# Two graph-attention layers on one core: masks of whole tiles compared in layer 0's stage, and layer 1's sums copied in one piece with the source of tiny weight as a row below the identity

## The chip, the cores and the metric

The kernel runs on one core of one Trainium2 chip. The metric is device time in microseconds, the median of several runs. Beside it there is one profiled execution with a trace of every engine: TensorE (PE, with its weight loads PEld), VectorE (DVE), ScalarE (ACT), GpSimd (POOL) and SyncE (SP), which here only issues transfers.

## The reference, cut to what matters

`x` is 2708 x 256 and `adj` 2708 x 2708, sparse, with a full diagonal; the rows and columns of low number hold the most entries. Layer 0 mixes each node's neighbours through attention heads and two gated cells. Layer 1, where the change is, is an attention over 4 heads of 64 channels:

```python
h = (x @ W).reshape(n, HEADS, C)
s_src = jnp.einsum('nhc,hc->nh', h, a_src)
s_dst = jnp.einsum('nhc,hc->nh', h, a_dst)
e = jax.nn.leaky_relu(s_src[:, None, :] + s_dst[None, :, :], NEG_SLOPE)
e = jnp.where((adj > 0.5)[:, :, None], e, MASK_VAL)
alpha = jax.nn.softmax(e, axis=0)
out = jnp.einsum('ijh,ihc->jhc', alpha, h).reshape(n, HEADS * C) + bias
...
x = _layernorm(x + out)
```

A node j with no `adj > 0.5` in its column gets the mean of all h, since its softmax is over equal values.

## The kernel before, in words

**Sparse tiles.** Columns of `adj` are cut into spans, 64 wide for layer 0 and 128 wide for layer 1 (22 spans, the last 20 wide). For each span a first stage finds which rows have an entry, and lists them. A span's work is a list of items: a few whole tiles (rows m x 128 to m x 128 + 127, taken as they lie, `WHOLE1`) and tiles of 128 listed rows, gathered by indirect transfers from POOL (`TILES1`). `work1` holds 111 items: 91 gathered and 20 whole ones, four of them for the first two spans, whose last two row blocks are taken whole.

**Layer 0's stage.** A loop over `work0` fetches `adj` values (`fetch_raw`) and rows of the table `T0` (`fetch_rows`), scales them (`prepared`), multiplies (`multiplied`), and after each 512 columns runs the gated cells and the normalization (`cells_and_norm`), which also writes rows of h, scaled by exp of the source's logit, to the table `T1`. At item 40 of this loop the masks of layer 1's gathered tiles are fetched too: `fetch_mask`, line 1231, gathers 128 x 128 of `adj` into one of six `raw1` buffers, and DVE compares it with 0.5 into `m1`, one byte an entry.

**Layer 1's stage.** For each item, `fetch_h` (line 1312) brings 128 rows of `T1`, and for a whole tile also 128 x 128 of `adj` over SP's queue. `weighed` (line 1325) compares that tile with 0.5 on DVE into a bf16 mask, and computes for each head the weights `q = max(S, row's value) * mask` with one `scalar_tensor_tensor`. `S` is a span's share of the destination's factor on all partitions, copied by ACT into PSUM (`near`, line 1302). `attended` multiplies on PE: for each head 128 rows x 65 columns of h (64 channels and the weight itself, so the 65th row of the product is the denominator) into one of four PSUM banks.

**The end of a span.** `finished` (line 1364): ACT moves the bank to SBUF with four activations (one a head), each adding a bias by partition, `least_h`: 1e-20 times the mean of h, and 1e-20 for the denominator. This is a source of tiny weight, which decides only for a node without neighbours. PE turns the four 65 x 128 pieces into 128 x 65 with transposes, DVE takes the reciprocals of the denominators (`den`), ACT scales (`y`, four pieces), and DVE and ACT do the residual and the normalization in turn (`less`, `var`, `f_rstd`, `away`), before SP stores 128 rows of the result.

**What sets the order.** Nothing is issued as the loops run. `Plan` (line 99) records every operation with what it reads and writes, gives it an assumed cost, and `issue` (line 230) then places the operations one after another on the engines, each time the ready one with the longest tail of work behind it. So each engine's queue is in the planner's order, and an operation added in one place can move others. [...] All lines of the profile read L219, since the planner issues everything from there; the names of the tiles tell the operations apart. Tiles cut from common memory show under its name: `f_home` stands for layer 0's large buffers and in layer 1's stage for `q`, `o` and `S`; `f_m` for `m1`; `m` also for a whole tile's mask; `pl` and `ls` for the PSUM copies of `S`; `side` for the two PSUM banks of short products.

`kept` (line 862) are three 128 x 512 tiles through which products of the first stage go to memory (`XH`); they are not used after the first 261 us.

Of the kernel before, what the change touches and what calls it, by code (L numbers as in the profile page):

```python
# [10 lines left out]
F32 = mybir.dt.float32  # L11
BF16 = mybir.dt.bfloat16
I32 = mybir.dt.int32
U8 = mybir.dt.uint8
AF = mybir.ActivationFunctionType
ALU = mybir.AluOpType
# [4 lines left out]
P = 128  # L21
D = 256
KD = D // P
HEADS0 = 3
HEADS1 = 4
C1 = D // HEADS1
# [4 lines left out]
CH = 512  # L31
# [6 lines left out]
LEAST1 = 1.0e-20  # L38
# [6 lines left out]
W1 = 128  # L45
# [263 lines left out]
def fast_path(ctx: ExitStack, tc: tile.TileContext, i: dict, out: bass.AP, bad: bass.AP):  # L309
# [11 lines left out]
    nc = plan = Plan(tc.nc)  # L321
    x, xT_in, adj, adjT = i["x"], i["xT"], i["adj"], i["adjT"]
# [3 lines left out]
    size = [min(P, N - b * P) for b in range(NB)]  # L326
# [7 lines left out]
    TW = D + 8  # L334
    C65 = C1 + 1
# [13 lines left out]
    const = ctx.enter_context(tc.tile_pool(name="f_const", bufs=1))  # L349
# [3 lines left out]
    def ring(tiles):  # L353

        return cycle(tiles).__next__
# [29 lines left out]
    ident = const.tile([P, P], F32, name="f_ident")  # L385
# [64 lines left out]
    for t, of in ((less_room, TILES0 + TILES1), (less_whole, WHOLE0 + WHOLE1)):  # L450
        c = 0
        while c < len(of):
# [4 lines left out]
            c = e  # L457

    least = const.tile([NB, 1], F32, name="f_least")
# [62 lines left out]
    w1 = const.tile([P, KD, D + 2 * HEADS1], F32, name="f_w1")  # L522
# [8 lines left out]
    idx1 = const.tile([P, len(TILES1), max(TILES1)], I32, name="f_idx1")  # L531
# [5 lines left out]
    m1 = const.tile([P, sum(TILES1), W1], U8, name="f_m1")  # L537
    small, lists = Rings(const, 2), Rings(const, 2)
# [117 lines left out]
    def gathered(dst, table, idx, at):  # L656
        nc.gpsimd.indirect_dma_start(
            dst, None, table, bass.IndirectOffsetOnAxis(ap=idx, axis=0), element_offset=at
        )

    work0, work1 = [], []
# [21 lines left out]
    def fetch_raw(n):  # L683

        c, whole, m = work0[n]
        d0, w = spans[0][c]
        home, at = raw_home(n)
        raws[n] = home[:, at * W0 : at * W0 + w]
        if whole:
            nc.sync.dma_start(raws[n], adjT[m * P : (m + 1) * P, d0 : d0 + w])  # L690
        else:
            gathered(raws[n], adjT, idx0[:, c, m : m + 1], d0)
# [11 lines left out]
    for h in range(HEADS0):  # L704
        for k in range(KD):
            nc.vector.scalar_tensor_tensor(
                junk, gat_w[:, h, k, :], 1.0, a_b[:, 2 * h * D : (2 * h + 1) * D],
                op0=ALU.mult, op1=ALU.mult, accum_out=uw[:, k, h : h + 1],
# [137 lines left out]


    kept_bank = ring([accs[1], dbs[1]])
    keptp = Rings(const, 3)

    def place_kept(g, n, o, gate):
        at = (((g * 2 + n) * KD + o) * 3 + gate) * P
# [21 lines left out]
    for g, cs in enumerate(groups):  # L874
        w = width[g]
        pe, pf = accs[0], dbs[0]
        c0, nf = base[g] // W0, w // W0
        for b0 in range(0, NB, 2):
# [13 lines left out]
            whole = size[b0 + 1] == P  # L892
# [11 lines left out]
            for b in pair:  # L904
                if b in cs:
                    p, o = size[b], b * P - base[g]
# [16 lines left out]
            for b in pair:  # L923
                p = size[b]
# [3 lines left out]
            for b in pair:  # L928
                p = size[b]
# [37 lines left out]
    rowp, sp = Rings(const, 9), Rings(const, 4)  # L967
# [4 lines left out]
    rows, ready = {}, {}  # L972
# [253 lines left out]
    slot1 = {}  # L1226
    for n, (c, whole, m) in enumerate(work1):
        if not whole:
            slot1[n] = len(slot1)

    def fetch_mask(n):
        c, whole, m = work1[n]
        d0, w = spans[1][c]
        r = small.tile([P, W1], F32, name="raw1", bufs=6)
        gathered(r[:, :w], adj, idx1[:, c, m : m + 1], d0)
        nc.vector.tensor_scalar(m1[:, slot1[n], :w], r[:, :w], 0.5, None, op0=ALU.is_gt)

    for n, (c, whole, m) in enumerate(work0):
        if n == EARLY:
            for k in slot1:  # L1240
                fetch_mask(k)
        fetch_raw(n)
        fetch_rows(n)
        prepared(n)
        if multiplied(n):
            divided(c)
            d0, w = spans[0][c]
            if d0 + w in (base[g] + width[g] for g in range(NG)):
                cells_and_norm(d0 // CH)
# [17 lines left out]
    qp, op = Rings(const, 4, home4), Rings(const, 2, home2[:, 4 * CH :])  # L1267
# [4 lines left out]
    xmean = const.tile([P, KD], F32, name="f_xmean")  # L1272
# [1 line left out]
    nc.vector.tensor_scalar(xmean, xmean, 1.0 / N, None, op0=ALU.mult)  # L1274


    least_h = const.tile([C65, HEADS1], F32, name="f_least_h")
    nc.vector.memset(least_h, LEAST1)
    pm = side()
    for h in range(HEADS1):  # L1280
        for k in range(KD):
            nc.tensor.matmul(
                pm[:C1, h : h + 1], lhsT=w1[:, k, h * C1 : (h + 1) * C1], rhs=xmean[:, k : k + 1],
                start=(k == 0), stop=(k == KD - 1), skip_group_check=True,
            )
    nc.vector.tensor_scalar(least_h[:C1], pm[:C1, :HEADS1], LEAST1, None, op0=ALU.mult)

    def on_all_partitions(g):
        S_b = next_S()
# [7 lines left out]


    near_bank = ring([pl_bank(), ls_bank()])

    def near(c):
        d0, w = spans[1][c]
# [7 lines left out]
    hrows, hready, outs, of_g, of_c = {}, {}, {}, {}, {}  # L1310

    def fetch_h(n):
        c, whole, m = work1[n]
        d0, w = spans[1][c]
        hg, r = rowp.tile([P, TW], F32, name="rows"), None
        if whole:
            p = size[m]
            r = small.tile([P, W1], F32, name="raw1")
            nc.sync.dma_start(hg[:p], T1[m * P : m * P + p, :])
            nc.sync.dma_start(r[:p, :w], adj[m * P : m * P + p, d0 : d0 + w])  # L1320
        else:
            gathered(hg, T1[: (NB - LATE) * P, :] if c < SPLIT else T1, idx1[:, c, m : m + 1], 0)
        hrows[n] = (hg, r)

    def weighed(n):
        c, whole, m = work1[n]
        d0, w = spans[1][c]
        late = whole and m >= NB - LATE
        if (c, late) not in of_c:
            of_c[c, late] = near(c)  # L1330
        S = of_c[c, late]
        hg, r = hrows[n]
        p = size[m] if whole else P
        if whole:
            mask = small.tile([P, W1], BF16, name="m2")[:p, :w]
            nc.vector.tensor_scalar(mask, r[:p, :w], 0.5, None, op0=ALU.is_gt)
        else:
            mask = m1[:, slot1[n], :w]
        q = qp.tile([P, HEADS1, W1], F32, name="q")
        for h in range(HEADS1):  # L1340
            nc.vector.scalar_tensor_tensor(
                q[:p, h, :w], S[:p, h, :w], hg[:p, H65 + h : H65 + h + 1], mask,
                op0=ALU.max, op1=ALU.mult,
            )
        hready[n] = q

    def attended(n):

        c, whole, m = work1[n]
        w = spans[1][c][1]  # L1350
        start = c not in outs
        stop = n == ends1[c]
        p = size[m] if whole else P
        if start:
            outs[c] = out_bank()
        q, hg = hready.pop(n), hrows.pop(n)[0]
        for h in range(HEADS1):
            nc.tensor.matmul(
                outs[c][:C65, h * W1 : h * W1 + w], lhsT=hg[:p, h * C65 : (h + 1) * C65], rhs=q[:p, h, :w],
                start=start and h == 0, stop=stop and h == HEADS1 - 1, skip_group_check=True,  # L1360
            )
        return stop

    def finished(c):
        p = size[c]
        o = op.tile([C65, HEADS1, W1], F32, name="o")
        out_c = outs.pop(c)
        for h in range(HEADS1):
            nc.scalar.activation(
                o[:, h, :p], out_c[:C65, h * W1 : h * W1 + p], AF.Identity, bias=least_h[:, h : h + 1]  # L1370
            )
        pt = side()
        for h in range(HEADS1):
            nc.tensor.transpose(pt[:p, h * C65 : (h + 1) * C65], o[:, h, :p], ident[:C65, :C65])
        got = pt[:p, :H65].rearrange("p (h c) -> p h c", h=HEADS1)
        den = small.tile([P, HEADS1], F32, name="den")
        nc.vector.reciprocal(den[:p].rearrange("p (h o) -> p h o", o=1), got[:, :, C1:])
        y = small.tile([P, HEADS1, C1], F32, name="y")
        for h in range(HEADS1):
            nc.scalar.activation(y[:p, h, :], got[:, h, :C1], AF.Copy, scale=den[:p, h : h + 1])  # L1380
        y = y[:p].rearrange("p h c -> p (h c)")

        less = small.tile([P, 1], F32, name="less")[:p]
        var = small.tile([P, 1], F32, name="var")[:p]
        away = small.tile([P, 1], F32, name="away")[:p]
        scale = rstd[:p, c : c + 1]
        nc.vector.scalar_tensor_tensor(
            xn[:p, c, :], xn[:p, c, :], 1.0, y, op0=ALU.mult, op1=ALU.add, accum_out=less
        )
        nc.vector.tensor_scalar(less, less, -1.0 / D, None, op0=ALU.mult)  # L1390
        nc.scalar.activation(y, xn[:p, c, :], AF.Square, bias=less, accum_out=var)
        nc.scalar.activation(scale, var, AF.Sqrt, bias=eps[:p], scale=1.0 / D)
        nc.vector.reciprocal(scale, scale)

        nc.vector.tensor_mul(away, less, scale)
        nc.scalar.activation(
            xn[:p, c, :], xn[:p, c, :], AF.Identity, bias=away, scale=scale
        )
        nc.sync.dma_start(out[c * P : c * P + p, :], xn[:p, c, :])
# [461 lines left out]
```

## Time and profile before

| | |
|---|---|
| median of 3 runs | 1038.06 us (1037.52 to 1051.02) |
| profiled execution | 877.66 us |
| its span, first to last instruction | 875.8 us |
| mean granted TensorE clock in it | 0.959 |
| PE, DVE, ACT, POOL busy | 780.4, 609.9, 551.3, 532.3 us |
| layer 1's stage | from about 715 us to the end |

The profiled execution is 160 us shorter than the median of the runs. In the profile's rows a busy time is followed by the mean length of one instruction in ns and then the idle time of the engine just before it with what ended it. Instructions overlap somewhat with the next on the same engine, so that a length is more than an instruction's share of the engine's time. In the timeline and the chain the first number is the start and the second the length, both in us.

### The profile page before, as it was taken

The numbers are of one execution on the slowest core, as the hardware profiler recorded it, in microseconds if no ns is written. First come the engines' busy times: TensorE is split into PE (matmuls) and PEld (weight loads), VectorE is DVE, ScalarE is ACT, GpSimd is POOL, SyncE is SP. The second block draws the span as 40 slices with busy tenths as digits, with TensorE's granted clock in tenths as the row PEclk, the third lists the DMA queues.
The fourth block names the chain that finished last, engine by engine and source line by source line (L and its number), as shares of the span: only waits on it lengthen the run. The fifth ranks groups of instructions, "written<-read, shape, count | busy, mean of one in ns | idle before, by whom it ended". The sixth has DMA issues, their size and how long they took to land. (4 is left out here: it accounts for less than half of the span.)

```text
span 875.8 us, 14092 instructions
## 1 busy us (share of the span) xinstructions
PE 780.4 (89%) x3911; PEld 490.4 (56%) x3911; DVE 609.9 (70%) x2063; ACT 551.3 (63%) x1560; POOL 532.3 (61%) x613
## 2 busy tenths in 40 slices
PE   4999998997999999988998997999999899998882
PEld 3533333444556764656555744754664588777761
DVE  6259585865846674978478638727857849999993
ACT  3368997975568885658456844745764432237887
POOL 3000557557667777777777777777776243677630
PEclk9989999998999999989999999999999799999995
DMA  9476887878683342453446425434534143565531
GB/s 345 135 236 209 277 263 241 288 242 243 204 235 98 106 128 56 135 147 105 112 143 198 126 65 159 126 96 118 159 103 123 29 141 94 172 187 171 169 98 53
DMA packets 88503, 138.71 MB, mean 158 GB/s; under 512 B 21904, under 2 KB 44264, under 8 KB 87776
## 3 DMA queue, kind: packets, MB, share of 16 engines
q1 hardware_dynamic: 67168, 90.56, 32.2%
q0 software_dynamic: 20320, 45.59, 19.7%
q10 hardware_dynamic: 928, 1.57, 0.5%
q8 instruction: 33, 0.54, 0.3%
q14 instruction: 54, 0.44, 0.2%
HBM read 116.18 MB, written 24.26 MB: 160 GB/s over the span
## 5 line engine op out<-in xcount | busy, mean ns | idle before, releaser
L219 POOL DMA_INDIRECT rows<-f_T,f_idx x254 | 258.0, 1016 | 115.9 <-PE acc L219 26.8
L219 PE MATMUL acc<-four,rows 128*128 128x256 f32 (+1 forms) x712 | 187.9, 400 | 8.8 <-ACT four L219 5.7
L219 ACT ACTIVATE four<-four,rows 128x64 f32<-128x64 f32 (+1 forms) x534 | 143.3, 336 | 23.0 <-DMA rows<-f_T,f_idx 15.8
L219 PEld LDWEIGHTS acc<-four,rows 128*128 128x128 f32 x712 | 131.6, 196 | 45.8 <-ACT four L219 14.2
L219 POOL DMA_INDIRECT raw<-in_adj_dram,f_idx x91 | 90.5, 995 | 40.7 <-DVE f_m L219 15.3
L219 POOL DMA_INDIRECT f_xn<-in_adjT_dram,f_idx x63 | 66.8, 1060 | 20.1 <-issue 16.6
L219 POOL DMA_INDIRECT f_home<-in_adjT_dram,f_idx x67 | 66.4, 991 | 20.3 <-issue 16.3
L219 PE MATMUL acc<-f_home,rows 128*65 128x128 f32 (+2 forms) x512 | 65.2, 279 | 3.9 <-ACT f_home L219 2.6
L219 DVE TENSOR_TENSOR f_home<-f_home,side 128x512 f32<-128x512 f32 (+1 forms) x64 | 41.9, 658 | 32.4 <-PE side L219 31.2
L219 PEld LDWEIGHTS acc<-f_home,rows 128*65 128x65 f32 (+1 forms) x512 | 55.7, 140 | 9.6 <-ACT f_home L219 3.5
L219 PE MATMUL side<-f_home,f_gat_w 128*128 128x512 f32 (+1 forms) x144 | 58.7, 569 | 2.0 <-DVE f_home L219 1.9
L219 PE MATMUL side<-f_home,f_node_wi 128*128 128x512 f32 (+1 forms) x144 | 59.1, 543 | 1.3 <-DVE f_home L219 1.3
L219 ACT ACTIVATE m<-four 128x64 bf16<-128x64 f32 (+1 forms) x181 | 40.2, 246 | 28.1 <-DVE four L219 24.0
L219 PE MATMUL side<-f_home,f_edge_wi 128*128 128x512 f32 (+1 forms) x144 | 57.4, 544 | 0.0
L219 DVE SCALAR_TENSOR_TENSOR f_home<-pl,rows,f_m 128x128 f32<-128x128 f32 x196 | 55.2, 335 | 0.0
L219 POOL DMA_INDIRECT f_m<-in_adjT_dram,f_idx x33 | 31.9, 967 | 37.3 <-DVE f_rel L219 20.1
L219 PE MATMUL db<-f_home,rows 128*65 128x128 f32 x376 | 48.8, 282 | 6.3 <-DVE f_home L219 4.0
L219 DVE SCALAR_TENSOR_TENSOR f_home<-ls,rows,f_m 128x128 f32<-128x128 f32 (+1 forms) x168 | 46.3, 331 | 2.8 <-DMA rows<-f_T,f_idx 1.7
L219 PEld LDWEIGHTS db<-f_home,rows 128*65 128x65 f32 x376 | 39.0, 137 | 13.9 <-DVE f_home L219 5.9
L219 DVE TENSOR_REDUCE f_found<-f_home 128x16 f32<-128x1024 f32 (+8 forms) x52 | 43.7, 860 | 3.3 <-POOL f_home L219 3.3
L219 ACT ACTIVATE f_home<-f_home,f_minus_half 128x1024 bf16<-128x1024 f32 (+5 forms) x44 | 41.9, 965 | 5.8 <-PE db L219 4.1
L219 PEld LDWEIGHTS side<-f_home,f_gat_w 128*128 128x128 f32 x144 | 28.0, 208 | 30.1 <-issue 27.1
(231 smaller groups left out, 1537.3 us busy)
## 6 DMA issues: line engine op xcount, KB each, us to landing
f_home<-in_adjT_dram SPq DMA_DIRECT2D x30, 512.0 KB
f_XH<-kept SPq DMA_DIRECT2D x60, 256.0 KB
f_home<-f_XH SPq DMA_DIRECT2D x60, 256.0 KB
f_node_wi<-in_adjT_dram SPq DMA_DIRECT2D x10, 512.0 KB
f_edge_wi<-in_adjT_dram SPq DMA_DIRECT2D x10, 512.0 KB
f_home<-f_TS SPq DMA_DIRECT2D x5, 1024.0 KB
rows<-f_T SPq DMA_DIRECT2D x33, 132.0 KB
rows<-f_T,f_idx POOLq DMA_INDIRECT x254
```

What stands on the lines that cost most here:

```text
L219: call = lambda: f(*args, **kwargs)
```

## The change

1. Masks of whole tiles: `fetch_mask` now runs for all 111 items of `work1`. For a whole tile it loads `adj` over SP's queue into the same six `raw1` buffers and compares into one byte an entry, in space cut from the `kept` tiles (now `kept_home`). `fetch_h` no longer loads `adj`, and `weighed` no longer compares.
2. Sums: `finished` copies the bank with one ACT copy of 65 x (4 x width) into one of two fixed `o` tiles, whose rows 64 to 95 are set to 1.0 beforehand. The copy overwrites row 64 and row 65 stays 1.0.
3. The source of tiny weight: `back_h` holds, for each head, the 65 x 65 identity and below it, in row 65, 1e-20 times the mean of h (and 1e-20 for the denominator). The transposes become plain products of `o` (66 rows) with `back_h` (66 rows), which turn the piece and add row 65 at once. The row is made as 1 x 256 by two products with `xmean` in place of eight, scaled by DVE into `least`, and brought to partition 65 by a transfer on SP's queue.

```diff
-    keptp = Rings(const, 3)
+    kept_home = const.tile([P, 3 * CH], F32, name="f_kept_home")
+    keptp = Rings(const, 3, kept_home)
...
+    m1_whole = [
+        kept_home[:, k * W1 // 4 : (k + 1) * W1 // 4].bitcast(U8) for k in range(len(work1) - len(slot1))
+    ]
+    masks1 = {}
+
     def fetch_mask(n):
         c, whole, m = work1[n]
         d0, w = spans[1][c]
-        r = small.tile([P, W1], F32, name="raw1", bufs=6)
-        gathered(r[:, :w], adj, idx1[:, c, m : m + 1], d0)
-        nc.vector.tensor_scalar(m1[:, slot1[n], :w], r[:, :w], 0.5, None, op0=ALU.is_gt)
+        p = size[m] if whole else P
+        r = small.tile([P, W1], F32, name="raw1", bufs=6)[:p, :w]
+        if whole:
+            nc.sync.dma_start(r, adj[m * P : m * P + p, d0 : d0 + w])
+            masks1[n] = m1_whole.pop()[:p, :w]
+        else:
+            gathered(r, adj, idx1[:, c, m : m + 1], d0)
+            masks1[n] = m1[:, slot1[n], :w]
+        nc.vector.tensor_scalar(masks1[n], r, 0.5, None, op0=ALU.is_gt)
...
-            for k in slot1:
+            for k in range(len(work1)):
                 fetch_mask(k)
...
-    least_h = const.tile([C65, HEADS1], F32, name="f_least_h")
-    nc.vector.memset(least_h, LEAST1)
+    back_h = op.tile([P, HEADS1, C65], F32, name="back_h", bufs=1)
+    nc.vector.memset(back_h[C1 : C1 + 32], LEAST1)
+    nc.vector.tensor_copy(
+        back_h[:C65], ident[:C65, :C65].rearrange("p (o c) -> p o c", o=1).to_broadcast([C65, HEADS1, C65])
+    )
     pm = side()
-    for h in range(HEADS1):
-        for k in range(KD):
-            nc.tensor.matmul(
-                pm[:C1, h : h + 1], lhsT=w1[:, k, h * C1 : (h + 1) * C1], rhs=xmean[:, k : k + 1],
-                start=(k == 0), stop=(k == KD - 1), skip_group_check=True,
-            )
-    nc.vector.tensor_scalar(least_h[:C1], pm[:C1, :HEADS1], LEAST1, None, op0=ALU.mult)
+    for k in range(KD):
+        nc.tensor.matmul(
+            pm[:1, :D], lhsT=xmean[:, k : k + 1], rhs=w1[:, k, :D], start=(k == 0), stop=(k == KD - 1)
+        )
+    least = op.tile([1, HEADS1, C65], F32, name="least_h", bufs=1)
+    nc.vector.memset(least, LEAST1)
+    nc.vector.tensor_scalar(
+        least[:, :, :C1], pm[:1, :D].rearrange("p (h c) -> p h c", h=HEADS1), LEAST1, None, op0=ALU.mult
+    )
+    nc.sync.dma_start(back_h[C65 : C65 + 1], least)
...
+    o_tiles = [op.tile([P, HEADS1, W1], F32, name=f"o{k}", bufs=1) for k in range(2)]
+    for o in o_tiles:
+        nc.vector.memset(o[C1 : C1 + 32], 1.0)
+    next_o = ring(o_tiles)
...
     def fetch_h(n):
-        hg, r = rowp.tile([P, TW], F32, name="rows"), None
+        hg = rowp.tile([P, TW], F32, name="rows")
         if whole:
             p = size[m]
-            r = small.tile([P, W1], F32, name="raw1")
             nc.sync.dma_start(hg[:p], T1[m * P : m * P + p, :])
-            nc.sync.dma_start(r[:p, :w], adj[m * P : m * P + p, d0 : d0 + w])
...
     def weighed(n):
-        if whole:
-            mask = small.tile([P, W1], BF16, name="m2")[:p, :w]
-            nc.vector.tensor_scalar(mask, r[:p, :w], 0.5, None, op0=ALU.is_gt)
-        else:
-            mask = m1[:, slot1[n], :w]
+        hg, mask = hrows[n], masks1[n]
...
     def finished(c):
-        o = op.tile([C65, HEADS1, W1], F32, name="o")
-        out_c = outs.pop(c)
-        for h in range(HEADS1):
-            nc.scalar.activation(
-                o[:, h, :p], out_c[:C65, h * W1 : h * W1 + p], AF.Identity, bias=least_h[:, h : h + 1]
-            )
+        o = next_o()
+        out_c = outs.pop(c).rearrange("p (h j) -> p h j", h=HEADS1)
+        nc.scalar.copy(o[:C65, :, :p], out_c[:C65, :, :p])
         pt = side()
         for h in range(HEADS1):
-            nc.tensor.transpose(pt[:p, h * C65 : (h + 1) * C65], o[:, h, :p], ident[:C65, :C65])
+            nc.tensor.matmul(
+                pt[:p, h * C65 : (h + 1) * C65], lhsT=o[: C65 + 1, h, :p], rhs=back_h[: C65 + 1, h, :],
+                start=True, stop=True, skip_group_check=True,
+            )
```

More of the change, by code (lines that the diff above doesn't have):

```diff
@@ L1314, in fetch_h @@
         d0, w = spans[1][c]
-        hg, r = rowp.tile([P, TW], F32, name="rows"), None
+        hg = rowp.tile([P, TW], F32, name="rows")
         if whole:
             p = size[m]
-            r = small.tile([P, W1], F32, name="raw1")
             nc.sync.dma_start(hg[:p], T1[m * P : m * P + p, :])
-            nc.sync.dma_start(r[:p, :w], adj[m * P : m * P + p, d0 : d0 + w])
         else:
             gathered(hg, T1[: (NB - LATE) * P, :] if c < SPLIT else T1, idx1[:, c, m : m + 1], 0)
-        hrows[n] = (hg, r)
+        hrows[n] = hg
     def weighed(n):
@@ L1331, in weighed @@
         S = of_c[c, late]
-        hg, r = hrows[n]
+        hg, mask = hrows[n], masks1[n]
         p = size[m] if whole else P
-        if whole:
-            mask = small.tile([P, W1], BF16, name="m2")[:p, :w]
-            nc.vector.tensor_scalar(mask, r[:p, :w], 0.5, None, op0=ALU.is_gt)
-        else:
-            mask = m1[:, slot1[n], :w]
         q = qp.tile([P, HEADS1, W1], F32, name="q")
@@ L1355, in attended @@
             outs[c] = out_bank()
-        q, hg = hready.pop(n), hrows.pop(n)[0]
+        q, hg = hready.pop(n), hrows.pop(n)
         for h in range(HEADS1):
```

## The prediction

> **What bounds the kernel now.** I read first the span in 40 slices, to see which engine is full where.
>
> ```profile
> PE   4999998997999999988998997999999899998882
> DVE  6259585865846674978478638727857849999993
> ACT  3368997975568885658456844745764432237887
> PEclk9989999998999999989999999999999799999995
> ```
>
> PE is full through layer 0. From slice 33 (about 720 us) on it is DVE, and in the last three slices ACT rises. The busy times by stage say it sharper (columns: PE, PEld, DVE, ACT, POOL busy, granted clock, DMA share, GB/s):
>
> ```profile
> 715.00:840.00 125.00, 112.95 (x947) 97.55 (x946) 122.71 (x525) 59.55 (x187) 79.22 (x83) 1.00 0.54 162
> 840.00:852.00 12.00, 10.14 (x88) 8.54 (x87) 11.90 (x65) 12.00 (x49) 2.15 (x2) 1.00 0.27 80
> 852.00:870.00 18.00, 5.39 (x29) 3.62 (x28) 7.42 (x44) 17.67 (x72) 0.00 (x0) 0.57 0.17 59
> ```
>
> DVE works 134.6 of the 137 us to 852, ACT only half of the first 125 us and then all of the last 30. So layer 1 has two limits in a row: DVE until about 840, ACT after that. The chain that ended last agrees: from 837 us on it is nearly all ACT.
>
> ```profile
> 844.47 0.48 ACT pl L219
> 845.48 0.26 ACT f_home L219 x2
> 845.82 0.67 ACT f_home L219 x2
> 861.70 0.96 ACT f_home L219 x4
> 868.67 1.00 ACT f_xn L219 x2
> ```
>
> Four bias activations of one column (`f_home`, 845.48 and 845.82) hold ACT 0.93 us, and those of the last column, only 20 wide (861.70), 0.96; one copy of 512 wide (`pl`) holds it 0.48. Then the groups of the stretch from 715 us, with the rows that the change touches:
>
> ```profile
> L219 DVE SCALAR_TENSOR_TENSOR f_home<-pl,rows,f_m 128x128 f32<-128x128 f32 x194 | 54.5, 334 | 0.0
> L219 ACT ACTIVATE f_home<-acc,f_least_h 65x128 f32<-65x128 f32 x44 | 12.7, 391 | 5.2 <-DVE f_least_h L219 3.6 <-PE side L219 1.6
> L219 PE MATMUL side<-f_ident,f_home 65*128 65x65 f32 x84 | 11.3, 252 | 8.3 <-ACT f_home L219 5.3 <-ACT y L219 2.9
> L219 DVE TENSOR_SCALAR m<-raw 128x128 bf16<-128x128 f32 x15 | 3.0, 205 | 0.0
> ```
>
> The transposes are recorded once each (84 for 21 columns)[...]; the other fp32 products are recorded twice. Last the timeline, for what an instruction really takes of its engine when others follow:
>
> ```profile
> 741.89 0.34 DVE L219 TENSOR_SCALAR m<-raw 128x128 bf16<-128x128 f32 x2
> 712.25 0.37 DVE L219 SCALAR_TENSOR_TENSOR f_home<-side,f_edge_bh,f_home 128x148 f32<-128x148 f32 x1 [7.58 <-PE side L219]
> 101.62 1.05 PE L219 MATMUL side<-f_sum,f_home 9*128 9x3 f32 x8
> 766.19 0.41 PE L219 MATMUL side<-f_ident,f_home 65*128 65x65 f32 x4
> 766.43 1.04 PE L219 MATMUL acc<-f_home,rows 128*65 128x128 f32 x8
> ```
>
> Two mask comparisons start at 741.89 and the next instruction at 742.16: 0.135 us each, not the 0.205 of the row. Four transposes take PE 0.24 us (766.19 to 766.43). And DVE stands idle 7.58 us before 712.25.
>
> [...] the eight records above, with 9 rows, 128 weight columns and only 3 moving ones, take (1.05 - 0.25)/7 = 0.114 us each[...]
>
> **Whole-tile masks.** 20 loads of `adj` and 20 comparisons leave `fetch_h` and `weighed` and go to `fetch_mask`. Three of the comparisons are before 715 us now and bound nothing. The other 17 are in the full DVE stretch: 17 x 0.135 = 2.3 us off. Reading a U8 mask (`f_m`, 334 ns) costs `scalar_tensor_tensor` what a bf16 one (`m`, 336 ns) does: nothing. DVE gains in that stretch one scaling of 1 x 256 for the row of tiny weight; by the 128 x 256 `tensor_scalar` (two in 0.72 us) some 0.35, against 0.14 for `f_least_h` today: +0.2. The memsets of `o` and `back_h` and the copy of the identity (five, at most 0.3 us each) stand in the new order ahead of the last group's cell, in the 7.58 us of idle time: 0, or 1 us if that idle goes. Net on DVE: -2.1.
>
> In layer 0 the 20 come on top: 2.7 us of DVE, which is 60 to 75% busy there, and on SP 20 issues of 0.33 us. PE is the bound there. But a comparison waits for its load[...]:
>
> ```profile
> DVE f_m L219 <- DMA raw<-in_adj_dram,f_idx: 33.0, 17, 9.5
> SPq L219 <- DMA raw<-in_adj_dram,f_idx: 19.8, 2, 15.5
> ```
>
> 33.0 us over 91 gathered masks is 0.36 each, so 20 x 0.36 = 7.3 us of DVE waits at most, behind which `four` and the cells' DVE work are queued and, behind these, PE. PE waited for DVE 21 us in all from 400 to 720 us, for all reasons. I take +0.5, bounds 0 and +7. A gain is possible only through a luckier order; -2. The first of the new comparisons must also follow the last store of a `kept` tile (DVE's last such copy is at 257.7 us, the comparison would be at about 261): at most 1 us, inside those bounds.
>
> **One copy for four bias activations.** 22 columns; the copy as `pl` above (the PSUM copies `kept` are 0.57 long, the same) at 0.48 against 0.97 with the gap between two: 0.49 less each. The columns before 840 us save ACT time that it has to spare: 0. After 840 us the timeline has 24 of the bias activations of 128 wide, six columns, and the last column's four, with ACT never idle: 6 x 0.49, and 0.96 less about 0.15 for a copy of 80 elements (the last `ls` copy holds ACT 0.12), is -3.7. Bounds: 0 (the columns' chains take over) and 22 x 0.49 = -10.8 (every column counts).
>
> **Products for transposes.** Each of 88 transposes (0.24/4 = 0.06) becomes a plain fp32 product with 66 rows, 128 weight columns, 65 moving: two records of 0.114, as `side<-f_sum`. A column takes 0.91 instead of 0.24 us, +0.67; 22 columns +14.7 us of PE. Up to 852 us that is beside DVE: an item (four heads) takes PE 0.87 (765.32 to 766.19), with a fifth of a column 0.92 now, 1.05 then; DVE takes 134.6/109 = 1.23. So cover is there at the profile's clock of 1.00, 0. In the tail PE is busy 5.4 of 18 us, though at clock 0.57; the new order has other ACT work of over 3 us between a column's copy and its `y`. I charge +0.3; +2 if every one of the last columns waits.
>
> **The row of tiny weight.** Two products instead of eight (-0.8 us of PE, hidden), then a store from SBUF to SBUF[...]. PE meets the first product that needs it four items, 3.5 us, after `xmean`'s. 0; +2 at most, and four `q` buffers cover DVE. The activations no longer wait for `f_least_h`, which came only at 762.1; that frees accumulator banks earlier: 0.
>
> **Sum.** -2.1 + 0.5 - 3.7 + 0.3 = -5.0, for the profiled execution 877.7 (span 875.8) to about 873. The median of the runs is 1038.06, 160 us above the profile, so those runs were under other conditions than the trace shows. Had everything followed TensorE's clock, 0.959 x 877.7/1038 = 0.81 would do it. I carry the difference over unscaled: 1033.1.
>
> **Rivals.**
> - *PE becomes layer 1's bound in the timed runs (slower).* At clock k PE needs 1.05/k an item, DVE 1.21: PE decides below k = 0.87; before the change below 0.92/1.23 = 0.75. [...] At 0.81, (1.30 - 1.23) x 109 = +7.6, with the tail's -3.4 +4.2; at 0.785 +9. Against it: in the trace the clock is 1.00 in this stretch. Some 1044 (1040 to 1048).
> - *Masks stall layer 0 (slower).* SP holds its queue up to 15.5 us for a ring slot already; with `f_XH` loads and `f_T` stores behind it once more, PE would miss about 10: +5, 1043 to 1048.
> - *The tail is not ACT's* but the last column's chain: -2.1 alone, +2 for the products: about 1038 (1037 to 1040).
> - *All of ACT's saving counts*, since columns finish earlier: -2.1 - 10.8 = -13: 1025.
>
> **Chances.** Forecast 0.47 (its own range 1029 to 1037), PE's bound 0.26, stalls 0.07, no gain 0.10, large gain 0.10. From 1025 to 1048 holds some 0.82. 2%, about what a measurement of this kernel can tell from no change, is 1017.3 and 1058.8: only a clock that differs between the runs, or bounds added up, lead there: 0.05 faster, 0.05 slower, 0.90 within.
>
> **What would show it.** Right: no `m<-raw` after 715 us; DVE's last full-width product about 1 to 2 us earlier; ACT copies of 65 x 512 near 0.5 us and its last piece 4 to 6 us earlier; `side` products in eight records a column. Wrong: PE's waits in layer 0 up by over 5 us, SP held longer by raw loads, or DVE idle for PE in layer 1.

## The result, and the profile after

The median went from 1039.59 us (4 runs, 1037.52 to 1051.02) to **1052.22 us** (4 runs, 1049.99 to 1055.13): ratio 1.0101, 95% interval 1.0057 to 1.0145. Forecast were 1033.1 us and a range to 1048. That is within 2% of no change, but of the other sign than forecast and outside the range.

Two things have to be known to read the numbers: both kernels take about 880 us on some chips and about 1035 to 1050 us on others, with nearly the same busy times of DVE and ACT, some 50 to 60 us more of PE and more idle time of all; and a ratio leaves out executions more than 1.5% above the fastest of their kernel, so that it isn't exactly the quotient of the medians beside it. The profile of the kernel before (877.66 us) is of the first kind, and all times of this first comparison, with the profile after (1049.99 us, span 1048.2), of the second. So these two profiles may not be subtracted.

The 40 slices of the changed kernel, as shown of before:

```profile
PE   4989796968688876987798859696988787988894
DVE  5376547546535551977267506642852756988895
ACT  4468676825347671656337614462563332242467
PEclk9789989987899988989998878898988979999897
```

Everywhere engines are emptier, PE too, and the mean granted clock is lower (0.888 against 0.959). The busy times show it by stage. I cut both profiles where DVE forms the mean of x (`f_xmean`), just ahead of layer 1's sums: at 742.7 us before and 903.4 us after (columns: PE, PEld, DVE, ACT, POOL busy, granted clock, DMA share, GB/s). Before:

```profile
0.00:742.70 742.70, 679.03 (x3069) 404.89 (x3069) 495.22 (x1541) 470.61 (x1275) 462.10 (x540) 0.97 0.54 161
742.70:842.70 100.00, 87.43 (x741) 74.34 (x740) 98.09 (x432) 53.69 (x179) 70.25 (x74) 1.00 0.58 171
```

After:

```profile
0.00:903.40 903.40, 729.28 (x3068) 425.21 (x3069) 500.94 (x1559) 470.63 (x1275) 453.97 (x540) 0.88 0.45 133
903.40:1003.40 100.00, 86.48 (x686) 77.12 (x685) 85.30 (x356) 36.61 (x102) 60.13 (x64) 0.95 0.47 142
```

Layer 0 is 160.7 us longer, 93% of the difference between the spans, with the same work on ACT (470.6 us) and nearly the same on DVE; PE is busy 50 us longer (729.3 against 679.0). The chain that ended last names what had no place in the chain before, idle time that nothing recorded ends:

```profile
PE 58%; another core or an unknown queue 9%; ACT 9%; DVE 8%; issue 7%; ACTq 0%; DVEq 0%
```

And the rows that the change touches, in the groups of after:

```profile
L219 DVE SCALAR_TENSOR_TENSOR f_home<-pl,rows,f_m 128x128 f32<-128x128 f32 x196 | 55.7, 340 | 5.7 <-PE acc L219 4.4 <-remote 0.8 <-PE side L219 0.4
L219 PE MATMUL side<-f_home 66*128 66x65 f32 x168 | 23.3, 284 | 9.0 <-ACT y L219 5.4 <-issue 3.2 <-ACT f_home L219 0.3
L219 ACT COPY f_home<-acc 65x512 f32<-65x512 f32 x11 | 6.4, 579 | 12.4 <-PE side L219 4.3 <-PE acc L219 4.3 <-PE db L219 3.8
L219 DVE TENSOR_SCALAR f_kept_home<-raw 128x128 uint8<-128x128 f32 x18 | 4.2, 241 | 2.0 <-issue 2.0
```

The change did what it says: one ACT copy a column, products of 66 rows with two records each, masks compared into `f_kept_home`. But DVE, never idle ahead of the first of these groups before, now waits 5.7 us ahead of it. The wait alone doesn't speak against the change: the kernel before waits there too in the longer condition, as a later profile of it (the control below) shows:

```profile
L219 DVE SCALAR_TENSOR_TENSOR f_home<-pl,rows,f_m 128x128 f32<-128x128 f32 x196 | 55.8, 340 | 7.3 <-PE acc L219 3.0 <-PE side L219 2.7 <-PE db L219 1.6
```

### The profile page after: what moved, and what is told of

Its sections match the earlier page's. It is cut to its first block, busy times and chain, and to the rows that moved or that the text cites. A ratio compares the mean times of both kernels' runs of the same rounds, so it can differ in the third digit from the quotient of the medians.

```text
span 1048.2 us, 14160 instructions
## 1 busy us (share of the span) xinstructions
PE 843.3 (80%) x3987; PEld 527.6 (50%) x3987; DVE 616.0 (59%) x2067; ACT 540.3 (52%) x1494; POOL 523.9 (50%) x613
## 4 chain that ended last, share of the span: by engine, by line
PE 58%; another core or an unknown queue 9%; ACT 9%; DVE 8%; issue 7%; ACTq 0%; DVEq 0%
PE acc L219 25%; PE side L219 18%; PE db L219 13%; DVE f_home L219 4%; ACT four L219 3%; PE pl L219 2%; ACT f_home L219 2%; ACT y L219 1%; DVE four L219 1%; ACT ids L219 1%; PE ls L219 1%; DVE f_xn L219 1%; ACT f_xn L219 1%; DVE ids L219 0%
## 5 line engine op out<-in xcount | busy, mean ns | idle before, releaser
L219 POOL DMA_INDIRECT rows<-f_T,f_idx x254 | 252.6, 994 | 218.4 <-issue 42.3
L219 PE MATMUL acc<-four,rows 128*128 128x256 f32 (+1 forms) x712 | 201.1, 422 | 14.6 <-ACT four L219 9.3
L219 PEld LDWEIGHTS acc<-four,rows 128*128 128x128 f32 x712 | 140.2, 208 | 55.3 <-issue 20.5
L219 PE MATMUL side<-f_home,f_edge_wi 128*128 128x512 f32 (+1 forms) x144 | 70.6, 641 | 40.8 <-ACT f_home L219 21.6
L219 PE MATMUL acc<-f_home,rows 128*65 128x128 f32 (+1 forms) x512 | 69.5, 288 | 6.4 <-issue 5.8
L219 PEld LDWEIGHTS side<-f_home,f_edge_wi 128*128 128x128 f32 x144 | 29.8, 222 | 78.2 <-issue 32.6
L219 PEld LDWEIGHTS acc<-f_home,rows 128*65 128x65 f32 (+1 forms) x512 | 59.1, 145 | 13.0 <-issue 8.2
L219 PE MATMUL side<-f_home,f_node_wi 128*128 128x512 f32 (+1 forms) x144 | 61.3, 558 | 3.0 <-DVE f_home L219 3.0
L219 PE MATMUL db<-f_home,f_only 128*22 128x512 bf16 (+2 forms) x132 | 39.2, 388 | 20.7 <-ACT f_home L219 17.8
L219 ACT ACTIVATE f_home<-f_home,f_minus_half 128x1024 bf16<-128x1024 f32 (+5 forms) x44 | 41.9, 965 | 24.9 <-issue 19.5
L219 POOL DMA_INDIRECT f_m<-in_adjT_dram,f_idx x33 | 31.6, 957 | 38.8 <-DVE f_rel L219 20.1
```

The source lines that it names most:

```text
L219: call = lambda: f(*args, **kwargs)
```

## The experiments

### The two halves, on a chip where the kernel before takes 880 us

First the kernel before itself, without an edit, to see which of the two conditions is its own.

> The kernel before, unchanged, once more with a trace. If the timed runs of before were under the conditions of the changed kernel's trace (span 1048, clock 0.89, stalls in which DVE, ACT and PE all stand), this trace shows them too: span near 1037, clock below 0.92. If those stalls belong to the change, they are absent here and the span is near 876.

It took 881.19 us, span 879.4, beside 43 timed runs with a median of 880.56, and none of its waits is put down to an unknown releaser. So 1038 us isn't the kernel's own time, but the chip's or the occasion's.

The masks alone (the hunks on `keptp`, `fetch_mask`, `fetch_h` and `weighed`):

```diff
-            for k in slot1:
+            for k in range(len(work1)):
                 fetch_mask(k)
...
-        if whole:
-            mask = small.tile([P, W1], BF16, name="m2")[:p, :w]
-            nc.vector.tensor_scalar(mask, r[:p, :w], 0.5, None, op0=ALU.is_gt)
```

> Only the masks of whole tiles are moved to layer 0's stage; the four bias activations and the transposes stay. Theory PE (the plain products cost it): no slower than before, ratio 0.995 to 1.000. Theory masks (the loads and comparisons stall layer 0): ratio 1.008 to 1.012, as the whole change. Theory order (any new order of the queues can cost or give a per cent): anything from 0.99 to 1.01.

876.17 us (22 runs) against 880.56: **0.9959** (0.9934 to 0.9984). The sums alone (the hunks on `back_h`, `o_tiles` and `finished`):

```diff
-        for h in range(HEADS1):
-            nc.scalar.activation(
-                o[:, h, :p], out_c[:C65, h * W1 : h * W1 + p], AF.Identity, bias=least_h[:, h : h + 1]
-            )
+        nc.scalar.copy(o[:C65, :, :p], out_c[:C65, :, :p])
```

> Only the sums in one copy, the plain products and the row of tiny weight; the masks of whole tiles stay in layer 1's stage. Theory PE: ratio 1.008 to 1.015. Theory masks: 0.995 to 1.000. Theory order: anything from 0.99 to 1.01.

876.70 us against 880.56: **0.9973** (0.9948 to 0.9999). Each half gains; neither costs. Last the whole change without its products:

```diff
+        nc.scalar.activation(o[:C65, :, :p], out_c[:C65, :, :p], AF.Identity, bias=tiny)
...
+            nc.tensor.transpose(pt[:p, h * C65 : (h + 1) * C65], o[:C65, h, :p], ident[:C65, :C65])
```

> The whole change, but PE keeps transposes: one activation with a constant bias of 1e-20 copies the sums, and there is no row of tiny weight. Left out: the mean of h for a node without neighbours. Theory PE: some 15 us of PE gone against the change, ratio to before 0.993 to 0.998. Theory masks: 1.005 to 1.010, nearly as slow as the change. Theory order: no sign foretold.

0.9824 (0.9782 to 0.9867), from six runs only (862.30 to 880.06 us), an unclear comparison. The median of all six, 871.79 us, is 0.990 of 880.56. It is repeated below.

### The whole change, and TensorE's part alone

> The changed kernel unchanged. Theory A (the stalls seen in its first profile are conditions, not its own): where the kernel before takes about 880 us, the two halves add up to 0.9959 x 0.9973 = 0.993 of it, 874 us, and no layer-0 wait of 10 us stands in the trace; layer 1 from the first mean to the end is 129 to 132 us against 133 before. Theory B (the order that results from both halves together stalls layer 0): a ratio of 1.005 or more also here, with waits of 10 us and more on VectorE and ScalarE at the same places as in the first profile.

873.86 us (22 runs) against 881.43: **0.9924** (0.9900 to 0.9947), as the halves multiply to 0.9932. The quotient of the medians, 0.991, is close to the 0.990 of the kernel with transposes above. No wait of 10 us in layer 0 stands without a recorded releaser. Here the profiles of one condition can be laid side by side. Layer 1 of the kernel before on this chip (`f_xmean` at 746.0), in its first 100 us and the rest:

```profile
746.00:846.00 100.00, 87.27 (x741) 74.20 (x740) 98.02 (x432) 53.55 (x178) 70.28 (x74) 1.00 0.58 171
846.00:879.40 33.40, 14.21 (x106) 11.31 (x104) 16.85 (x94) 27.25 (x109) 0.00 (x0) 0.68 0.17 56
```

And of the changed kernel (`f_xmean` at 739.5):

```profile
739.50:839.50 100.00, 96.10 (x808) 85.19 (x806) 98.45 (x428) 47.72 (x140) 70.47 (x74) 1.00 0.57 167
839.50:868.10 28.60, 13.89 (x114) 12.91 (x114) 14.53 (x82) 21.71 (x81) 0.00 (x0) 0.72 0.17 57
```

Layer 1 is 4.8 us shorter (33.4 to 28.6 after its first 100 us). ACT has 5.5 us less to do in that rest, DVE 2.3, and in the first 100 us DVE stays full. TensorE's busy time has come close to DVE's: 96.1 beside 98.5 us, where it was 87.3.

TensorE's part alone is the kernel before with one edit:

```diff
-            nc.tensor.transpose(pt[:p, h * C65 : (h + 1) * C65], o[:, h, :p], ident[:C65, :C65])
+            nc.tensor.matmul(
+                pt[:p, h * C65 : (h + 1) * C65], lhsT=o[:, h, :p], rhs=ident[:C65, :C65],
+                start=True, stop=True, skip_group_check=True,
+            )
```

> The kernel before with one edit: plain products of 65 rows with the identity in place of the transposes, no other part of the change. The prediction's step 4 (TensorE's extra 0.67 us per column, 15 us in all, is hidden beside VectorE at full clock): ratio 1.000 to 1.003, with TensorE's busy time 10 to 16 us above the kernel before. The rival (TensorE becomes layer 1's bound where its clock falls): 1.005 to 1.015, and VectorE's idle time in layer 1 is ended by a TensorE product.

881.36 us against 881.43: **1.0002** (0.9979 to 1.0026), with TensorE's busy time at 796.5 us against 783.5. Layer 1's first 100 us:

```profile
745.50:845.50 100.00, 93.61 (x791) 86.39 (x791) 96.40 (x421) 51.90 (x169) 68.63 (x73) 0.97 0.57 168
```

So TensorE is busy 13 us longer and the time doesn't move. The counterpart takes the products out of the changed kernel, and brings the row in by one bf16 product:

```diff
+            nc.tensor.transpose(pt[:p, h * C65 : (h + 1) * C65], o[:C65, h, :p], ident[:C65, :C65])
+        nc.tensor.matmul(
+            pt[:p, :H65], lhsT=ones_h[:1, :p], rhs=least, start=False, stop=True, skip_group_check=True
+        )
```

> The change with its masks and its one copy, but the transposes kept, and the tiny weight added by one bf16 product of one row that accumulates onto them. Step 4 of the prediction: as the plain products are hidden, the same time as the changed kernel within 0.3%. The rival on TensorE: 0.5 to 1.0% faster than the changed kernel, about 0.985 of the kernel before, as the kernel with the transposes and a constant in ScalarE's operation gave 0.982 in an unclear comparison.

This kernel doesn't give the reference's sums (why is not shown), so only its time is read. 874.99 us, **0.9924** (0.9897 to 0.9952), the ratio of the changed kernel to the fourth digit. Both edits say the same: at 880 us plain products cost nothing that these intervals, about 2.5 us to either side, can show.

### The condition of the first comparison, met on a second chip

> The changed kernel unchanged, beside the kernel without the row and the plain products. Where the kernel before takes about 880 us: 0.990 to 0.995, as in the run before. Where it takes about 1040 us (the condition of the first comparison): 1.005 to 1.015 if the first comparison is a property of that condition, 0.990 to 0.997 if it was an accident of few runs.

Here the kernel before took 1036.37 us (43 runs, 1019.91 to 1051.73). The changed kernel took 1032.17 us (22 runs, 1020.87 to 1046.70): **0.9988** (0.9949 to 1.0027; the quotient of the medians is 0.996). The first comparison was not repeated. Beside it ran the kernel without row and products:

> The kernel of the run with masks moved, one ScalarE operation with a constant and the transposes kept (it leaves out the mean of h for a node without neighbours, and with it the row of tiny weight, its two products and its store), once more with more rounds, as its first comparison was unclear at 0.982. Theory A (steps 4 and 5 of the prediction: the plain products and the row of tiny weight cost nothing): the ratio of the changed kernel, 0.990 to 0.994. Theory B (the row and the products cost 5 to 9 us at the start or the end of layer 1): 0.980 to 0.985, the changed kernel beside it at 0.990 or more.

1028.38 us, 0.9967 (0.9935 to 0.9999). This overlaps the changed kernel's interval. Its median is 3.8 us below the changed kernel's, so here a cost of row and products of that size is neither shown nor excluded. The unclear 0.9824 could not be repeated, as this run met the other condition.

### A control without an edit, and two more chips at 880 us

A comparison of the kernel before with itself says what an interval is worth. These six runs were meant for the longer condition and met the shorter on two other chips.

> The kernel before, once more as if it were another kernel: no edit at all. It measures what a comparison says of no change. Theory A (runs that wait 10 us and more for nothing that the program shows scatter alike for every load of a kernel): 0.997 to 1.003. Theory B (each load of a kernel has an offset of its own, which four or five runs of one load share): a ratio up to 1% off, above all where the kernel before takes about 1040 us.

> The changed kernel unchanged, beside that control. By the runs so far: 0.990 to 0.995 where the kernel before takes about 880 us, 0.995 to 1.003 where it takes about 1040. A second value near 1.010 would say that the first comparison is a property of the kernel in some condition, not an accident.

> The kernel before with plain products in place of the transposes. At about 880 us it was 1.0002. Where the kernel before takes about 1040 us and the granted clock is lower, the rival that names TensorE as layer 1's bound wants 1.005 to 1.015; the forecast, by which these 15 us of TensorE are hidden, 0.997 to 1.003.

> The control once more (the kernel before as if it were another kernel), for the condition in which it takes about 1040 us. Theory A (the waits scatter alike for every load of a kernel): 0.996 to 1.004. Theory B (each load has its own offset there): up to 1% off. At about 880 us it says nothing new: 1.000.

> The changed kernel beside the control. At about 1040 us: 0.995 to 1.003 by the one comparison with many runs in that condition; a value of 1.006 to 1.014 would repeat the first comparison, and then the change costs something in some sessions that its trace at 870 us does not show.

> The kernel before with plain products for the transposes, for the condition of about 1040 us. The rival (TensorE becomes layer 1's bound at the lower clock): 1.005 to 1.015. The forecast (hidden): 0.997 to 1.003.

| | first chip | second chip |
|---|---|---|
| control, no edit | 1.0010 (0.9982 to 1.0038) | 0.9996 (0.9971 to 1.0021) |
| changed kernel | 0.9877 (0.9820 to 0.9935) | 0.9886 (0.9835 to 0.9936) |
| products alone | 1.0003 (0.9968 to 1.0037) | 0.9990 (0.9957 to 1.0024) |

The changed kernel has six runs in each, hence the wide intervals. The control stays at 1, the products too, the change gains.

### The control in the longer condition

> The control (the kernel before as if it were another), again for the condition of about 1040 us, where it also gives the length of layer 1 in the kernel before. If it takes about 1040 us: 0.996 to 1.004 if the scatter there is the same for every load, up to 1% off if each load has its own offset; layer 1 then 148 to 151 us, as the changed kernel has 143 to 145 there. At about 880 us: 1.000 and 133 to 135.

> The changed kernel beside it. About 1040 us: 0.995 to 1.003, or near 1.010 if the first comparison is a property of the kernel there. About 880 us: 0.988 to 0.993, layer 1 at 127 to 129 us.

On this chip the kernel before took 1033.98 us (43 runs). The control gave **1.0001** (0.9969 to 1.0033), the changed kernel 1028.92 us (22 runs, 1015.45 to 1041.76), **0.9920** (0.9887 to 0.9953; the quotient of the medians is 0.995). So two loads of one kernel don't differ by 1% here, and the change gains here as well. The windows of the kernel before (control) on this chip, layer 0 and layer 1:

```profile
0.00:883.50 883.50, 729.69 (x3069) 427.28 (x3069) 496.90 (x1541) 471.56 (x1275) 457.64 (x540) 0.90 0.45 136
883.50:1029.80 146.30, 107.56 (x843) 89.93 (x842) 116.20 (x524) 81.30 (x285) 70.28 (x74) 0.89 0.44 129
```

And of the changed kernel on the same chip:

```profile
0.00:893.90 893.90, 730.50 (x3068) 427.03 (x3069) 498.97 (x1560) 470.19 (x1275) 462.20 (x540) 0.89 0.45 135
893.90:1035.40 141.50, 112.16 (x922) 101.53 (x919) 114.65 (x509) 69.50 (x220) 69.89 (x74) 0.93 0.43 129
```

Layer 1 is 4.8 us shorter here too, in one profile of each. Layer 0 is 10 us longer in this pair, but the profiled execution of the changed kernel (1037.22 us) is 8.3 us above that kernel's median, and the control's (1031.61) 0.8 below its own: single executions scatter that much. The longest waits of DVE in layer 0, in the control (DVE's timeline, idle time and releaser in brackets):

```profile
231.37 0.89 DVE L219 TENSOR_TENSOR ids<-f_home,f_places 128x1408 bf16<-128x1408 bf16 x1 [13.45 <-remote]
402.62 0.69 DVE L219 TENSOR_TENSOR f_home<-f_home,side 128x512 f32<-128x512 f32 x1 [12.93 <-remote]
617.19 0.69 DVE L219 TENSOR_TENSOR f_home<-f_home,side 128x512 f32<-128x512 f32 x1 [20.36 <-issue]
```

In the changed kernel on the same chip:

```profile
231.11 0.89 DVE L219 TENSOR_TENSOR ids<-f_home,f_places 128x1408 bf16<-128x1408 bf16 x1 [13.61 <-remote]
406.76 0.69 DVE L219 TENSOR_TENSOR f_home<-f_home,side 128x512 f32<-128x512 f32 x1 [11.29 <-remote]
616.74 0.69 DVE L219 TENSOR_TENSOR f_home<-f_home,side 128x512 f32<-128x512 f32 x1 [20.46 <-remote]
711.67 0.69 DVE L219 TENSOR_TENSOR f_home<-f_home,side 128x512 f32<-128x512 f32 x1 [23.49 <-remote]
```

And in the profile of the first comparison's result:

```profile
236.17 0.89 DVE L219 TENSOR_TENSOR ids<-f_home,f_places 128x1408 bf16<-128x1408 bf16 x1 [13.76 <-remote]
417.53 0.69 DVE L219 TENSOR_TENSOR f_home<-f_home,side 128x512 f32<-128x512 f32 x1 [13.05 <-remote]
629.46 0.69 DVE L219 TENSOR_TENSOR f_home<-f_home,side 128x512 f32<-128x512 f32 x1 [20.63 <-remote]
723.60 0.69 DVE L219 TENSOR_TENSOR f_home<-f_home,side 128x512 f32<-128x512 f32 x1 [23.18 <-remote]
```

The first three waits are in both kernels, at the same instructions and of much the same length. They aren't made by the change. The fourth is in the three profiles of the changed kernel (16.7 to 23.5 us) and in the one without row and products (25.0), so these two don't make it. In the one profile of the kernel before, DVE waits 9.7 us at 704.8 for a gathered mask and then 6.5 at 711.6, ahead of an instruction of that kind: 16.2 in two pieces. As the medians of this chip differ by -5 us, it can't be 20 us of cost; one profile doesn't tell whether it is some.

The last run asked whether the products are hidden in the longer condition, and met the shorter once more:

> The kernel before with plain products in place of the transposes, on a chip where the kernel before takes about 1035 us if it is one. The rival (TensorE becomes layer 1's bound at the lower clock): 1.005 to 1.015, and VectorE's idle time in layer 1 is ended by products of TensorE. The forecast (hidden): 0.996 to 1.004. At about 880 us it says nothing new: 0.998 to 1.002.

883.26 us against 881.48: 1.0022 (0.9994 to 1.0050). Of the kernel with the products alone there is no run in the longer condition.

## Why the prediction was wrong, step by step

Two pieces of layer 1 tell the parts of the change from each other: from `f_xmean` to the end of DVE's last full-width product, where DVE was to save, and from there to the end of the span, where ACT was to save (us, from the timelines; number of profiles in brackets).

| | to DVE's last full-width product | from there to the end |
|---|---|---|
| 880 us: kernel before (4) | 109.1 to 111.2 | 23.8 to 24.1 |
| products alone (4) | 108.5 to 112.2 | 24.0 to 25.5 |
| masks alone (1) | 108.0 | 24.5 |
| sums alone (1) | 110.8 | 19.7 |
| changed kernel (3) | 107.8 to 108.1 | 19.5 to 20.5 |
| longer condition: kernel before (1) | 122.9 | 23.4 |
| longer condition: changed kernel (3) | 122.0 to 125.2 | 19.5 to 19.9 |

**Masks, -2.1: right.** In the changed kernel at 880 us the last comparison into `f_kept_home` is at 687.6 us, none is in layer 1. The first piece went from 109.3 (the middle of four; 109.1, 109.3, 109.3, 111.2) to 107.8: some -1.5 us, near the forecast, and it did so with the masks alone and not with the sums alone. The 1 x 256 scaling holds DVE 0.33 us (estimated 0.35). Of the four memsets two of 32 x 512 are 0.49 us long and two of 260 wide 0.28 (0.3 at most was said); the row below merges them, and they stand in idle time as forecast:

```profile
705.77 1.75 DVE L219 MEMSET f_home<- 32x512 f32 x4 [4.09 <-PE side L219]
...
741.51 0.40 DVE L219 TENSOR_SCALAR f_home<-side 1x256 f32<-1x256 f32 x1
741.84 2.14 DVE L219 SCALAR_TENSOR_TENSOR f_home<-pl,rows,f_kept_home 128x128 f32<-128x128 f32 x8
```

**Masks in layer 0, +0.5 with bounds -2 and +7: right, nearer the lower end.** The waits on `raw` (what waited for it, us and times) in the changed kernel:

```profile
  DVE f_m L219: 21.3, 20
...
  DVE f_kept_home L219: 2.1, 1
```

The new comparisons wait 2.1 us in all, where 7.3 was the bound, and those of the gathered masks wait 12 us less than the 33.6 of the kernel before on that chip. Masks alone gained 0.4%, 4.4 us, of which layer 1 shows about 1; the rest would have to be layer 0's, but its length scatters from 742 to 748 us in four profiles of the kernel before, so that isn't shown.

**One copy, -3.7: right.** ACT in the tail of the changed kernel at 880 us:

```profile
847.75 0.58 ACT L219 COPY f_home<-db 65x512 f32<-65x512 f32 x1
848.21 0.31 ACT L219 ACTIVATE f_rstd<-var,f_eps 128x1 f32<-128x1 f32 x1
...
853.58 0.26 ACT L219 COPY f_home<-acc 65x80 f32<-65x80 f32 x1
853.69 0.57 ACT L219 ACTIVATE y<-f_xn,less 128x256 f32<-128x256 f32 x1
```

A copy holds ACT 0.46 us and the last 0.11 (0.48 and 0.15 were taken), six columns and the last are in the tail, and the second piece went from 23.8 to 24.1 us to 20.5, 20.1 and 19.5: -3.9, where -3.7 and the products' +0.3 make -3.4. It is as short with the sums alone, as long as before with the masks or the products alone, and 3.5 to 3.9 us shorter in the longer condition too. The rivals "all of ACT's saving counts" (-13) and "the tail is not ACT's" (0) fall.

**Products, 0 up to the tail: right at 880 us.** In the tail a column's eight records take PE 0.94 us (0.91 taken):

```profile
847.91 1.11 PE L219 MATMUL side<-f_home 66*128 66x65 f32 x8 [0.31 <-ACT y L219]
848.85 1.04 PE L219 MATMUL acc<-f_home,rows 128*65 128x128 f32 x8
```

The working had PE at 1.05 us of DVE's 1.23 an item, 85%; the busy times above say 96.1 of 98.5 us. That doesn't refute it, since a busy time counts eight products to the end of the last, 1.04 us, while the next eight can start after 0.87. By the records in that stretch (683 products of items and 120 of columns), at 0.87 and 0.94 us for eight, I estimate 88 us, 90% of DVE's 98.5. DVE's waits say it more plainly: in eleven profiles at 880 us, of the kernel before, the changed one and the products alone, DVE waits for PE ahead of the weights `q` of layer 1 for 0.6 us at most. With the four comparisons of the products alone (1.0002, 1.0003, 0.999, 1.0022) they are hidden there.

**The row of tiny weight, 0: right at 880 us.** In the changed kernel's profile the store is issued at 741.94 us and PE starts the first product of a column at 745.34, straight after other products; no wait is put down to the store. No trace shows when it landed: how long the store takes, and with it the bound of +2, was the author's estimate.

**TensorE as the bound at a lower clock: fallen as put.** The rival's clock of 0.81 was an estimate from the ratio of the times (its sum at 0.785 is +8.3, not +9); that PE's time goes as 1/k was another. In layer 0 it went about so: PE is busy 729.7 us in the control of the longer condition against 679.0 in the profile before, 1.075 times as long, at a mean clock of 0.90 against 0.97 (0.97/0.90 is 1.078). A clock that stays near 0.81 is not shown: in the profiles of before and after of the first comparison the clock's records hold only 1.0 and 0.5. In the latter its mean is 0.95 in layer 1's first 100 us and 0.85 in the rest, where PE is busy 27.5 of 44.8 us. But PE isn't hidden in the longer condition in any of the three kernels profiled there: DVE waits for it ahead of the weights `q` 9.9 us in the one profile of the kernel before, 11.3 to 11.9 in the three of the changed kernel and 4.7 in the one without row and products. So the first piece of layer 1 shows no gain from the masks there (table), and whether the products cost some of it is not shown.

**Sum, -5.0: right.** Measured are -7.6, -6.6 and -9.4 us of medians on the three chips at 880 us, and -4.2 and -5.1 on the two at 1035. Layer 1 alone: 133.1, 133.4, 135.0 and 133.2 us before, 128.6, 127.9 and 127.3 after, -5.8; in the longer condition 146.3 before and 141.5, 143.3 and 144.8 after.

**The step that failed: "I carry the difference over unscaled: 1033.1."** The difference carries over where many runs are compared: -4.2 and -5.1 us of medians on the two chips of the longer condition. The base held too (1038.06, then 1039.59). What failed is the term that the step put at nothing: how much the 160 us differ from one occasion and one execution to the next. They don't stay the same. Layer 0 took 883.5 us in the kernel before and 891.7, 893.9 and 903.4 in the changed kernel, in four profiles of that condition; executions of the changed kernel spread by 26 us there on one chip, and the three on record for the kernel before by 13.5; the forecast's own range was 8 wide. Four runs of each then gave +12.6 us where -5 was said.

I named "other conditions" and then reasoned only on a clock. The control shows what they consist of. Its layer 0 is 140.8 us longer than in the profile before: PE is busy 50.7 us more (729.7 against 679.0, at a mean clock of 0.90 against 0.97) and idle 90.1 us more. So PE at a lower clock can be a third of it, not all; whether the waits lower the clock or the reverse is not shown.

**What stays open.** The first comparison's +12.6 us. By its profile the excess is in layer 0: 903.4 us against 891.7 and 893.9 for the same kernel on the other two chips of the condition, while layer 1 has 144.8 against 143.3 and 141.5. Scatter as on those chips isn't enough: none of the 44 runs there reached its lowest, 1049.99. That something of that chip or occasion added to it is a guess; whether it adds to the kernel before alike is not known, since four and four runs, three of them from earlier, are all there is. That the change costs 1% in general is excluded by five comparisons on five chips.

## What to carry to other kernels

When the profiled execution and the timed runs differ by far more than the change is worth, find what the difference consists of before adding a forecast to the slower time, and widen the range by what it scatters. Here, laid against a profile of the same length, about two thirds of it (90.1 of 140.8 us in layer 0) was idle time of TensorE, part of that waits at the same instructions in both kernels, and one third (50.7 us) TensorE busy for longer. Compare lengths of stages, and of pieces of them, between profiles of one condition: a saving of 5.8 us was plain there (133.7 to 127.9 us), piece by piece and half by half, and is easily lost in a total that scatters by 26 us. And when an engine's work is called hidden, look at the waits of the engine that it is to hide beside: ahead of its weights VectorE waited for TensorE 0.6 us at most in layer 1 at 880 us, and 5 to 12 us in the longer condition, in each of the three kernels profiled there.

## What was not expected of the hardware

The same kernel, the one before, had medians of 880.3 to 881.5 us on three chips and of 1034.0 and 1036.4 on two others, and the mean time of a DMA packet was much the same in the two profiles of the first comparison (83.6 ns in the one of 877.66 us, 83.8 in the one of 1049.99). In the longer condition DVE, ACT and PE stood still together, in the changed kernel's profile beside the control for example from 603 to 616 us, while POOL issued gathers up to 612.8. Such stretches of over 1 us, after the first 60 us, add up to 48 us in the control and 66 us in that profile, and to 4 us in one profile of each kernel at 880 us. The trace of the first comparison's result holds fewer than half the semaphore updates of the one before (8,439 against 18,404), so "remote" may only mean that the record is lost. Whether the recording takes part in the waits, or something else on those chips, no run here tells.
